# The second feed-forward's down projection: a two-level split into 49 products in place of a one-level split into 7

## The chip, the core and the metric

The kernel runs on one core of one Trainium2 chip, alone. The metric is the device time of one execution in microseconds. TensorE (PE) multiplies, VectorE (DVE) and ScalarE (ACT) work on vectors out of SBUF and PSUM, GpSimd (POOL) does vector work out of SBUF, and SyncE (SP) issues most of the DMAs. In the profile PEld is the load of TensorE's stationary operand, which has a row of its own.

## The reference

Everything is float32. There are 8 sequences of 512 tokens with 512 features, and a context of 64 rows a sequence. Two layers are computed, each a gated attention to the context and a gated feed-forward:

```python
x = x + tanh(g_xattn[0]) * linear_attention(layernorm(x), ctx, Wq, Wg, bg, Wkv, Wo)
x = x + tanh(g_ffn[0]) * (gelu(layernorm(x) @ proj1.T + b1) @ proj2.T + b2)          # 512 -> 2048 -> 512
x = x + tanh(g_xattn[1]) * softmax_attention(layernorm(x), ctx, mask)
# the second feed-forward: 8 experts of width 192, all of them used, weighted per token by a router
w_tg = top8_of_softmax_summed_by_group(layernorm(x) @ gate_weight.T)                  # token x expert
act  = silu(h_gate) * h_up          # h = layernorm(x) @ gate_up_proj[dominant].T
x = x + tanh(g_ffn[1]) * sum_g w_tg[:, g] * (act[:, g] @ down_proj[g].T)              # 512 -> 8*192 = 1536 -> 512
```

The change concerns the last line: per sequence a product of 512 x 1536 activations (already weighted by the router) with a 1536 x 512 matrix.

## The kernel before

The work runs in three phases of eight sequences each (`b` = 0 to 7): `xa0` (linear attention), `ff0` (first feed-forward) and `ff1` (second attention and second feed-forward). While the products of one sequence run, the preparation of the next (layer norm, transposes, in `ff1` also the whole second attention and the router) is fed in between, a step at a time; it is a generator, `prep`.

**Split products.** A matrix product is cut into 2 x 2 blocks on each side and done as seven block products in place of eight, with sums and differences of blocks formed beforehand (Strassen's scheme in Winograd's form). The seven are numbered 1 to 7; `ORDER = (1, 2, 6, 5, 7, 4, 3)` is the order in which they are issued. `Unit.step(m)` issues product `m` and then what follows it (`after`). Products add up in PSUM: `BANK` gives each one of three banks, x, w or z, and those in `OPENS` start a bank afresh. `steps` issues the last two products of a unit (4 and 3) only behind the first product of the next unit, so that other engines have time.

**Up units.** `Ff1Up` makes 256 columns of each of the four blocks of the activation; there are six per sequence, `i` = 0 to 5. Each of its seven products is four matmuls with 128 x 128 weights held and 256 tokens moving (L711). Even units fill the blocks `a11` and `a21`, odd ones `a12` and `a22`. After an odd unit `combine_inner` forms `s1`, `s2` and the new `a21` for these columns.

**Down unit.** `Down` is the unit of the change. For sequence `b` in `ff1` it has 6 chunks, so each of its seven products is 12 matmuls: 128 x 128 of the activation held, 256 columns of the weights moving (L823). `after` adds the bank straight into the residual `xb` with one DVE operation of 512 elements (L839), and updates `s2` after product 6 (L842).

**Weights.** The block combinations of the weights are the same for all sequences. They are formed once by `build_weights` on POOL and kept in DRAM (`store`), for `ff1` during the `ff0` phase. Tiles of 128 x 512 (256 KB) come back through a ring of 16 buffers in SBUF. Their loads stand on SP's queue in the order of use, 16 tiles ahead, each waiting for PE to be done with the buffer that it takes.

**What sets the order.** In `ff0` and `ff1` a scheduler of the language orders the instructions of each engine; each engine then runs its own in that order. PSUM has eight banks: three for `ps` (transposes and the like), five for the units' sums.

Of the kernel before, what the change touches and what calls it, by code (L numbers as in the profile page):

```python
# [30 lines left out]
P = 128  # L31
# [12 lines left out]
H2 = 256  # L44
# [24 lines left out]
def flamingo_kernel(  # L69
# [41 lines left out]

    def acc_bank(name):
        return bank["acc"].tile([P, 2, H2], F32, tag="acc", name=name)
# [149 lines left out]
    def order_gate():  # L263
# [9 lines left out]

    store = {
        (ph, kind, i, q): dram.tile([P, 2, H2], F32, tag=f"{ph}_{kind}{i}_{q}", name=f"{ph}_{kind}{i}_{q}")
        for ph, kind, n in (("ff0", "up", 4), ("ff0", "down", 4), ("ff1", "up", 6), ("ff1", "down", 3))
# [58 lines left out]
    def build_weights(ph, tile7):  # L335

        todo = {
            "ff0": (("up", raw_p1, 4), ("down", raw_p2, 4)),
            "ff1": (("up", raw_gu, 6), ("down", raw_dn, 3)),
        }[ph]  # L340
        todo = [(kind, raw, i) for kind, raw, n in todo for i in range(n)]

        def load(kind, raw, i):
            t = tile7(f"{ph}_{kind}{i}")
            raw(t, i)
            return t

        t = load(*todo[0])
        yield
        for n, (kind, raw, i) in enumerate(todo):  # L350
            following = load(*todo[n + 1]) if n + 1 < len(todo) else None
            yield from combining(nc.gpsimd, t)
            for q in range(7):
                nc.sync.dma_start(out=store[ph, kind, i, q], in_=t[q])
            yield
            t = following


    def normed(ph, b, tag):
# [26 lines left out]
        def turn(t):  # L386
            pt = psum(f"pt_{tag}_{t}").rearrange("p (c q) -> p c q", q=P)
            for c in range(NC):
                nc.tensor.transpose(pt[:, c, :], xn[t][:, ts(c, P)], ident)  # L389
            nc.scalar.copy(xnT[:, :, ts(t, P)], pt)  # L390
# [196 lines left out]
    def prep_ff1(b):  # L587
# [54 lines left out]
        for i in range(2):  # L642
            spread_share(b, i)
# [24 lines left out]
    OPENS = (1, 5, 2)  # L668

    class Unit:  # L670


        banks: dict

        def step(self, m):
            name = BANK[m]
            if m in OPENS:
                self.banks[name] = acc_bank(f"{name}_{self.tag}")
            self.product(m, self.banks[name])
            self.after(m, self.banks[name])  # L680

# [8 lines left out]
    class Up(Unit):  # L690
        kind = "up"

        def __init__(self, ph, b, i):
            self.ph, self.b, self.i, self.tag = ph, b, i, f"{ph}_{b}_{i}"
            self.banks, self.s = {}, {}
# [78 lines left out]

    class Ff1Up(Up):


        def part(self, r, c, p, s):
            if (r, c) == (1, 1):
                if self.i == 0:  # L780
                    open_inner("ff1", self.b, NJ // 2)
                self.g = {}
# [15 lines left out]
            else:  # L798
# [3 lines left out]
                if r == 2:  # L802
                    self.up22 = u
                else:
                    nc.vector.tensor_tensor(h, u, self.g[1], ALU.mult)
                    if self.i % 2:
                        combine_inner(ts(self.i // 2, 2))

    class Down(Unit):
        kind, i, prefix = "down", 0, ""  # L810

        def __init__(self, ph, b, chunks):
            self.ph, self.b, self.chunks, self.tag, self.banks = ph, b, chunks, f"{ph}_{b}_down", {}

# [15 lines left out]
        def after(self, m, p):  # L830

            xb = xs[self.ph, self.b]
            parts = {1: (1, 1), 2: (1, 1), 6: (1, 2), 7: (2, 2), 4: (2, 1), 3: (1, 2)}
            todo = [(parts[m], p)] if m in parts else []
            if m == 7:
                todo.append(((2, 2), self.banks["w"]))
            for (r, c), src in todo:
                dst = xb[:, ts(r - 1, 2), ts(c - 1, H2)]
                nc.vector.scalar_tensor_tensor(dst, src, GATE[self.ph], dst, ALU.mult, ALU.add)  # L839
            if m == 6:  # L840
                s2, a12 = self.inner["s2"], self.inner["a12"]
                nc.vector.tensor_tensor(s2, a12, s2, ALU.subtract)  # L842
            if m == 3:
                stores.append((self.ph, self.b))

# [119 lines left out]
    def steps(units, late=late):  # L965

        for u in units:
            for m in ORDER[:5]:
                yield u, m
                if m == 1:  # L970
                    yield from late
                    late.clear()
            late.extend((u, k) for k in ORDER[5:])
# [137 lines left out]
    def units_of(ph, b):  # L1111
        if ph == "ff0":
            return [Ff0Up(ph, b, i) for i in range(4)] + [Down(ph, b, NF // 2)]
        return [Ff1Up(ph, b, i) for i in range(6)] + [Down(ph, b, NJ // 2)]

    later = []
# [8 lines left out]
    def load_steps():  # L1125
        for u, m, _ in plan:
            key = (u.ph, u.kind, u.b, u.i, m)
            ring_w[key] = []
            for i in [u.i] if u.kind == "up" else range(u.chunks // 2):
# [3 lines left out]
                yield  # L1133

# [3 lines left out]
    for u, m in [*steps([ODown(B - 1)]), *late]:  # L1138
# [7 lines left out]
        acc=stack(tc.tile_pool(name="ff_acc", bufs=5, space=PSUM, reuse_waits="tile")),  # L1146
    )
    hpool = stack(tc.tile_pool(name="inner", bufs=1, reuse_waits="tile"))
# [16 lines left out]

    def build_tiles(name):
        t = buildp.tile([P, 7, 2, H2], F32, tag="build", name=f"build_{name}")
        return [t[:, q] for q in range(7)]
# [10 lines left out]
    for u, m, n in plan:  # L1179
        if n != at:  # L1180
# [5 lines left out]
            at, k, held = n, 0, False  # L1186
        u.step(m)
        for _ in range(1 if u.kind == "up" else u.chunks // 2):
            next(loads, None)
        k += 1  # L1190
        if k == 6:
            flush()
        if u.kind == "up" and u.ph == "ff1" and m == 5 and u.i < 4:
            spread_share(u.b, u.i + 2)
# [9 lines left out]
        if held:  # L1204
            if u.kind == "down" and u.b == work_list[n][1] and m == 2:
# [6 lines left out]
        if k * count // until > (k - 1) * count // until:  # L1212
            held = next(prep, None) == "last"
    flush()
    build.close()
# [44 lines left out]
```

## Time and profile before

| | |
|---|---|
| median of 3 runs | 2147.32 us (2147.06 to 2150.36) |
| the profiled execution's own time | 2149.09 us |
| its span, first to last instruction | 2147.3 us |
| PE matmul busy | 2116.5 us, 99% |
| PE weight load busy | 1798.6 us, 84% |
| DVE busy | 1068.6 us, 50% |
| ACT busy | 523.1 us, 24% |
| POOL busy | 225.9 us, 11% |
| DMA | 397.49 MB, mean 185 GB/s |

The last down projection of `ff1` ends with its matmuls at 2142 us, followed by one DVE operation and two stores of 256 KB. The granted clock of TensorE is 0.997 of full speed on average. Matmuls are pipelined: the record of one overlaps the next, so that time per matmul is read from the distance of starts, while the sum of a group counts overlaps once.

### The profile page before, as it was taken

To read this page: it belongs to the slowest core of one execution; us is meant where nothing else is said; L and a number is where in the kernel's file an instruction comes from. 1 tells how busy PE (TensorE), PEld (TensorE's weight loads), DVE (VectorE), ACT (ScalarE), POOL (GpSimd) and SP (SyncE) were. 2 spreads that over 40 slices of the span, in tenths; PEclk is the share of its full clock that TensorE was granted. 3 is DMA by queue.
4 is the path that set the end of the run, shared out by engine and by line. 5 is a ranking of instruction groups with operands and counts; after the bars stand their busy time and mean duration, and the time that the engine had idled before them with its cause. 6 is when DMAs were issued, how large, how long until landed. Compare 5 with 4: busy or idle time off the path is not lost.

```text
span 2147.3 us, 28078 instructions
## 1 busy us (share of the span) xinstructions
PE 2116.5 (99%) x10444; PEld 1798.6 (84%) x10444; DVE 1068.6 (50%) x1915; ACT 523.1 (24%) x1082; POOL 225.9 (11%) x216
## 2 busy tenths in 40 slices
PE   8999999999999999999999999999999999999998
PEld 4778787788888888888888888888888888888887
DVE  3687787543432324232334373747465573746453
ACT  3433333212130303132233221212121221213020
POOL 3121111332310101000000010100000010100000
PEclk9999999999999999999999999999999999999999
DMA  7345634699965655655555656565565666565662
GB/s 222 118 152 164 202 121 113 216 322 325 310 201 152 187 169 170 190 150 189 152 175 172 192 169 213 162 213 173 182 203 176 198 184 192 155 198 157 200 183 84
DMA packets 223880, 397.49 MB, mean 185 GB/s; under 512 B 32257, under 2 KB 54049, under 8 KB 219649
## 3 DMA queue, kind: packets, MB, share of 16 engines
q1 hardware_dynamic: 216304, 368.93, 55.2%
q10 hardware_dynamic: 5856, 23.20, 3.0%
q0 software_dynamic: 1584, 3.57, 0.7%
q8 instruction: 84, 1.38, 0.3%
q14 instruction: 52, 0.42, 0.1%
HBM read 335.97 MB, written 59.64 MB: 184 GB/s over the span
## 4 chain that ended last, share of the span: by engine, by line
PE 83%; issue 8%; DVE 3%; DMA 3%; POOL 1%; SPq 1%; ACT 1%; POOLq 0%; ACTq 0%
PE x_ff L711 25%; PE x_ff_down L823 18%; PE w_ff L711 13%; PE w_ff_down L823 9%; PE z_ff L711 6%; PE z_ff_down L823 5%; PE pt_ff L389 1%; PE pt_xa L389 1%; PE pr L580 1%; PE pst L538 1%; SPq L60 1%; PE x_q L711 1%; DMA w_v<-in_wkv 1%; PE x_xa_down L823 1%; POOL raw_ff_up L60 0%
## 5 line engine op out<-in xcount | busy, mean ns | idle before, releaser
L723 ACT COPY u_ff<-x_ff 128x512 f32<-128x512 f32 x240 | 139.8, 583 | 851.9 <-PE x_ff L711 851.7
L711 PE MATMUL w_ff<-S_ff,w_ff_up 128*128 128x256 f32 x1280 | 304.3, 380 | 0.0
L711 PE MATMUL x_ff<-S_ff,w_ff_up 128*128 128x256 f32 x1280 | 303.6, 380 | 0.6 <-ACT u_ff L723 0.6
L823 PE MATMUL x_ff_down<-w_ff_down,a_ff 128*128 128x256 f32 x1344 | 298.1, 379 | 0.8 <-DVE x_ff L839 0.8
L711 PE MATMUL x_ff<-xnT_ff,w_ff_up 128*128 128x256 f32 x1280 | 294.9, 380 | 0.0
L823 PEld LDWEIGHTS x_ff_down<-w_ff_down,a_ff 128*128 128x128 f32 x1344 | 255.2, 190 | 35.9 <-DVE x_ff L839 1.2
L711 PEld LDWEIGHTS x_ff<-xnT_ff,w_ff_up 128*128 128x128 f32 x1280 | 240.5, 190 | 38.0 <-issue 5.9
L711 PEld LDWEIGHTS w_ff<-S_ff,w_ff_up 128*128 128x128 f32 x1280 | 240.2, 190 | 38.0 <-issue 6.7
L711 PEld LDWEIGHTS x_ff<-S_ff,w_ff_up 128*128 128x128 f32 x1280 | 239.1, 190 | 35.6 <-issue 3.1
L823 PE MATMUL w_ff_down<-w_ff_down,s_ff 128*128 128x256 f32 x896 | 198.6, 379 | 0.0
L823 PEld LDWEIGHTS w_ff_down<-w_ff_down,s_ff 128*128 128x128 f32 x896 | 170.2, 190 | 23.1
L711 PE MATMUL z_ff<-xnT_ff,w_ff_up 128*128 128x256 f32 x640 | 151.8, 379 | 0.0
L839 DVE SCALAR_TENSOR_TENSOR x_ff<-x_ff_down,gates,x_ff 128x512 f32<-128x512 f32 x32 | 24.0, 752 | 231.6 <-PE x_ff_down L823 231.6
L711 PEld LDWEIGHTS z_ff<-xnT_ff,w_ff_up 128*128 128x128 f32 x640 | 119.3, 190 | 15.0
L839 DVE SCALAR_TENSOR_TENSOR x_ff<-x_ff_down,gates_half,x_ff 128x512 f32<-128x512 f32 x32 | 24.0, 751 | 164.9 <-PE x_ff_down L823 164.9
L823 PE MATMUL x_ff_down<-w_ff_down,s_ff 128*128 128x256 f32 x448 | 99.3, 379 | 0.0
L823 PE MATMUL z_ff_down<-w_ff_down,a_ff 128*128 128x256 f32 x448 | 99.3, 379 | 0.0
L823 PEld LDWEIGHTS x_ff_down<-w_ff_down,s_ff 128*128 128x128 f32 x448 | 85.1, 190 | 11.6
L823 PEld LDWEIGHTS z_ff_down<-w_ff_down,a_ff 128*128 128x128 f32 x448 | 85.1, 190 | 11.6
L766 DVE TENSOR_TENSOR a_ff<-w_ff,u_ff 128x512 f32<-128x512 f32 x64 | 43.8, 685 | 102.4 <-ACT u_ff L723 100.3
L801 DVE TENSOR_TENSOR up_ff<-w_ff,u_ff 128x512 f32<-128x512 f32 x96 | 66.0, 687 | 37.4 <-ACT u_ff L723 37.4
L510 POOL TENSOR_TENSOR x_ff<-x_ff,b_sb 128x512 f32<-128x512 f32 x28 | 35.9, 1286 | 422.9 <-DVE xn_ff L382 368.7
(221 smaller groups left out, 2491.0 us busy)
## 6 DMA issues: line engine op xcount, KB each, us to landing
w_ff_up<-ff_up SPq DMA_DIRECT2D x560, 256.0 KB
w_ff_down<-ff_down SPq DMA_DIRECT2D x392, 256.0 KB
x_ff<-x_ff SPq DMA_DIRECT2D x16, 1024.0 KB
share<-shares SPq DMA_DIRECT2D x64, 256.0 KB
ff_up<-build_ff_up SPq DMA_DIRECT2D x42, 256.0 KB
spread<-over SPq DMA_DIRECT2D x32, 256.0 KB
x_ff<-x_xa ACTq DMA_DIRECT2D x8, 1024.0 KB
x_ff<-x_ff ACTq DMA_DIRECT2D x8, 1024.0 KB
```

The costliest lines, as they stand in the source:

```text
L60: made = f(*args, **kw)
L389: nc.tensor.transpose(pt[:, c, :], xn[t][:, ts(c, P)], ident)
L510: nc.gpsimd.tensor_tensor(xb[:, t, :], xb[:, t, :], b2_sb, ALU.add)
L538: nc.tensor.matmul(pst[ts(r, M), :], lhsT=ctxT[:, c, :], rhs=xnT[:, c, :].rearrange("p (u r q) -> p r u q", u=2, r=2)[:, r], start=c == 0, ...
L580: nc.tensor.matmul(pr, lhsT=eT[half, t // 2, :], rhs=c2[half, :], start=True, stop=True)
L711: nc.tensor.matmul(p[:, n, :], lhsT=w[:, c, ts(n, P)], rhs=moving, **self.mark(m, 2 * n + c),)
L723: nc.scalar.copy(self.s[m], p)
L766: nc.vector.tensor_tensor(h, p, s, ALU.add)
L801: nc.vector.tensor_tensor(u, p, s, ALU.add)
L823: nc.tensor.matmul(p[:, t, :], lhsT=a[:, k, ts(t, P)], rhs=w[k // 2][:, k % 2, :], **self.mark(m, 2 * k + t),)
L839: nc.vector.scalar_tensor_tensor(dst, src, GATE[self.ph], dst, ALU.mult, ALU.add)
```

## The change

In `ff1` the down unit becomes `SplitDown`. Each of its seven block products is itself cut into 2 x 2 quarters and done as seven products of quarters: 49 in all, of three matmuls each, with 128 x 128 of the activation held and 128 columns of weights moving.

- Each inner product has 128 columns of PSUM of its own; the seven of an outer product lie side by side in two banks, four and three. The outer sums are made on these seven separately: in PSUM along x and w, and otherwise in a tile `sums`, filled by ACT (`first`) and added to by DVE (`more`).
- The inner scheme's last sums and the addition into the residual are made once per sequence, by `whole`: three additions and eight operations into `xb`, put off (`pending`) and issued four per step. In the last sequence they are done in three parts.
- The activation's quarters are combined by DVE right before each outer product: `combine(m)`, four operations of 384 elements, into two buffers `split`. `combine(1)` is called in two places.
- The outer products come in the order 2, 4, 1, 6, 5, 7, and 3 behind the next unit's first product. The units of `ff1` come odd first, `FF1_UNITS`, since products 2 and 4 use `a12` and `a22`. Tokens of the normed input are placed in another order, so that the quarters come out right.
- The weights are one DRAM tensor, `stream`, in order of use: 147 blocks of 128 x 128 for each sequence, read as 37 ring tiles where there were 21. `build_stream` makes it on POOL: three tiles with four operations of 512 elements as before and four of 896 more, and 21 stores in pieces of 512 bytes.
- The five banks of the units' sums have fixed numbers, and are handed out in the order in which they fall idle.

```diff
+    SPLIT_ORDER = (2, 4, 1, 6, 5, 7, 3)
+    SPLIT_INNER = (1, 2, 4, 5, 6, 7, 3)
+    SPLIT_CHUNKS = NJ // 4
+    stream = dram.tile([P, 7, 7, SPLIT_CHUNKS, P], F32, tag="stream", name="stream")
...
+    def build_stream(tile7):
+        place = [SPLIT_ORDER.index(m) for m in (1, 5, 2, 3, 6, 7, 4)]
+        for i in range(SPLIT_CHUNKS):
+            t = tile7(f"ff1_down{i}")
+            w = [t[k] for k in place]
+            raw_dn(w, i)
+            yield
+            yield from combining(nc.gpsimd, w)
+
+            t = buildp_view(t)
+            more = buildp_view(tile7(f"ff1_split{i}"))
+            m = {
+                1: t[:, :, 0, 0], 5: t[:, :, 0, 1], 2: t[:, :, 1, 0], 3: t[:, :, 1, 1],
+                6: more[:, :, 0, 0], 7: more[:, :, 0, 1], 4: more[:, :, 1, 0],
+            }
+            for dst, a, b in ((7, 3, 5), (5, 5, 1), (6, 3, 5), (4, 2, 6)):
+                nc.gpsimd.tensor_tensor(m[dst], m[a], m[b], ALU.subtract)
+                yield
+            for n, k in enumerate(SPLIT_INNER):
+                nc.sync.dma_start(out=stream[:, :, n, i, :], in_=m[k])
+            yield
...
+            at = t % 2 * 2 + t // 2 if tag.startswith("ff1") else t
+            nc.scalar.copy(xnT[:, :, ts(at, P)], pt)
...
+    FF1_UNITS = (1, 0, 3, 2, 5, 4)
...
+    class SplitDown(Unit):
+        kind, i = "down", 0
+        order, head = SPLIT_ORDER, 6
+        BANK = {2: "z", 4: "v", 1: "x", 6: "x", 7: "x", 5: "w", 3: "w"}
+        OPENS, CLOSES = (2, 4, 1, 5), (2, 4, 7, 3)
+        NAMES = {1: "a11", 2: "a12", 4: "a22", 5: "s1", 6: "s2", 7: "a21", 3: "s2"}
...
+        def combine(self, m):
+            a = self.quarters(m)
+            s = second.tile([P, 4, self.chunks, P], F32, tag="split", name=f"split{m}_{self.tag}", bufs=2)
+            nc.vector.tensor_tensor(s[:, 0], a["21"], a["22"], ALU.add)
+            nc.vector.tensor_tensor(s[:, 1], s[:, 0], a["11"], ALU.subtract)
+            nc.vector.tensor_tensor(s[:, 2], a["11"], a["21"], ALU.subtract)
+            nc.vector.tensor_tensor(s[:, 3], a["12"], s[:, 1], ALU.subtract)
+            self.combined[m] = s
+
+        def product(self, m, p):
+            a, s = self.quarters(m), self.combined.pop(m)
+            w = ring_w[self.ph, self.kind, self.b]
+            operand = {1: a["11"], 2: a["12"], 4: a["22"], 5: s[:, 0], 6: s[:, 1], 7: s[:, 2], 3: s[:, 3]}
+            for n, k in enumerate(SPLIT_INNER):
+                for c in range(self.chunks):
+                    at = (SPLIT_ORDER.index(m) * 7 + n) * self.chunks + c
+                    nc.tensor.matmul(
+                        p[n // 4][:, n % 4, :],
+                        lhsT=operand[k][:, c, :],
+                        rhs=w[at // 4][:, ts(at % 4, P)],
+                        start=m in self.OPENS and n % 4 == 0 and c == 0,
+                        stop=True,
+                        skip_group_check=True,
+                    )
+
+        def after(self, m, p):
...
+            def first(part):
+                nc.scalar.copy(self.sums[part][:, 0:4], p[0])
+                nc.scalar.copy(self.sums[part][:, 4:7], p[1][:, 0:3])
+
+            def more(part):
+                for at, src in ((slice(0, 4), p[0]), (slice(4, 7), p[1][:, 0:3])):
+                    dst = self.sums[part][:, at]
+                    nc.vector.tensor_tensor(dst, src, dst, ALU.add)
+
+            if m in (2, 4, 6, 5):
+                first({2: (1, 1), 4: (2, 1), 6: (1, 2), 5: (2, 2)}[m])
+            if m == 7:
+                more((2, 2))
+                more((2, 1))
+            if m in (1, 3):
+                more({1: (1, 1), 3: (1, 2)}[m])
+            if m == 6:
+                nc.vector.tensor_tensor(inner["s2"], inner["a12"], inner["s2"], ALU.subtract)
...
+        def whole(self, r, c):
...
+            return [
+                onto(6, 1), out_of(1, 0, 0), out_of(2, 0, 0), onto(5, 6), out_of(5, 0, 1), out_of(3, 0, 1),
+                out_of(5, 1, 1), out_of(7, 1, 1), onto(7, 6), out_of(7, 1, 0), out_of(4, 1, 0), done,
+            ]
...
-        return [Ff1Up(ph, b, i) for i in range(6)] + [Down(ph, b, NJ // 2)]
+        return [Ff1Up(ph, b, i) for i in FF1_UNITS] + [SplitDown(ph, b, NJ // 4)]
...
         u.step(m)
-        for _ in range(1 if u.kind == "up" else u.chunks // 2):
+        for _ in range(tiles_of(u, m)):
             next(loads, None)
+        for _ in range(4):
+            if pending:
+                pending.pop(0)()
+        if isinstance(u, Ff1Up) and u.i == FF1_UNITS[-1]:
+            if m == 2:
+                down_of[u.b].combine(2)
+                down_of[u.b].combine(4)
+            if m == 3:
+                down_of[u.b].combine(1)
+        if isinstance(u, SplitDown) and m in (4, 1, 6, 5, 7):
+            u.combine(SPLIT_ORDER[SPLIT_ORDER.index(m) + 1])
```

## The prediction

> **What bounds the kernel now.** I read the page first: its busy rows, then the chain.
>
> ```profile
> PE 2116.5 (99%) x10444; PEld 1798.6 (84%) x10444; DVE 1068.6 (50%) x1915; ACT 523.1 (24%) x1082; POOL 225.9 (11%) x216
> ...
> PE 83%; issue 8%; DVE 3%; DMA 3%; POOL 1%; SPq 1%; ACT 1%; POOLq 0%; ACTq 0%
> ...
> q1 hardware_dynamic: 216304, 368.93, 55.2%
> ```
>
> TensorE (PE) is busy for 99% of the span and carries the chain. Only PE time, or a new wait of PE, moves the end. The waits of PE in the second feed-forward (from 1216 us) come to one line, in the last batch:
>
> ```profile
> PE x_ff_down L823 <- DVE x_ff L839: 0.8, 1, 0.8
> ```
>
> Then the PE timeline of one down projection (ff1, the fourth of eight), and that of the kernel's first microseconds:
>
> ```profile
> 1428.34 1.89 PE L711 MATMUL x_ff<-xnT_ff,w_ff_up 128*128 128x256 f32 x8
> 1430.07 5.34 PE L823 MATMUL x_ff_down<-w_ff_down,a_ff 128*128 128x256 f32 x24
> 1435.25 5.34 PE L823 MATMUL w_ff_down<-w_ff_down,s_ff 128*128 128x256 f32 x24
> 1440.43 0.60 PE L389 MATMUL pt_xa<-ident,xn_xa 128*128 128x128 f32 x4
> 1440.87 1.46 PE L711 MATMUL z_ff<-xnT_ff,w_ff_up 128*128 128x256 f32 x6
> ...
> 1.07 2.93 PE L60 MATMUL idle<-zeros 128*128 128x128 f32 x12 [1.07 <-DVE heads L60]
> 3.79 1.06 PE L60 MATMUL pctx<-ident,ctx 128*128 128x128 f32 x4
> ```
>
> Every product written in the code runs as two passes (12 matmuls of a down product are x24, six idle ones x12); a transpose runs as one. From 1430.07 to 1435.25 are 5.18 us for 24 passes: 215.8 ns a pass of 256 columns. The starts count, since a row's length includes a drain that overlaps the next. Four transposes of 128 columns take 0.44 us, 109 ns each, and each loads its own 128x128 weights.
>
> **The products.** Per batch 84 products of 256 columns (7 of 12) become 147 of 128 columns (49 of 3). Before: 7 x 5.18 = 36.26 us. After: 294 passes, and the question is what a pass of 128 columns costs when each needs a fresh load of 128 columns. The load's record is 190 ns, longer than the whole 109 ns. But at 1440.00 us such a load starts 2 ns after the matmul before it, is on record to 1440.19, and the next matmul starts on its 215.8 ns: it lies beside the matmul. Whether it fits beside a matmul half as long is shown by the idle row: plain products with plain loads of 128 columns, each spaced 213 ns by their starts. The transposes pctx just behind them are spaced (1.06 - 0.42) / 3 = 213 ns too, against 109 at 1440 us, so PE ran there at half speed (512-column passes start 853 ns apart at 10 us, 429 ns at 18 us), and the load hid completely. At full speed that is 107 to 109 ns. Bounds: 107, and 190 if the load's whole record were bare. I take 109.3: 294 x 0.1093 = 32.13 us. Saved: 4.13 us a batch, **33.0 us** over eight. (At 110 ns it would be 31.4.)
>
> One rule speaks against this. The Trainium skill, "TensorE: Matmul & The Clock Gate", Part 3, says that a weight load overlaps running matmuls only where its row group differs; all rows here use all 128 rows. With that page's 107 ns a load, load and matmul in series would be an estimated 214 ns a pass and the change some 210 us slower. The trace disagrees already for 256 columns, as the load that starts 2 ns behind its matmul shows.
>
> **DVE work added.** Rows of ff1: tensor_tensor 128x256 425 ns, 128x512 685, 128x1536 1748, scalar_tensor_tensor 128x512 751. So 384 columns take about 555. In the DVE timeline independent 512-column operations start 600 ns apart (83 ns overlap), and one that needs the operation just before it 720; for 384 columns 470 and 590. Per batch: eight combinations of four operations, though only seven are used (the code forms that of product 1 twice: behind the last up unit and again behind product 4), 8 x 2.0 = 16 us; eight additions out of PSUM, 4.6; the outer sums, three additions and eight scalar_tensor_tensor, 7.2; less seven old ones, 5. That is some 23 us, two thirds of it in the down projection itself. There DVE has room, as the stretch of the same down projection shows (columns: PE, PEld, DVE, ACT, POOL busy, clock, DMA share, GB/s):
>
> ```profile
> 1398.99:1440.43 41.44, 41.44 (x194) 36.43 (x192) 14.79 (x21) 1.77 (x3) 0.00 (x0) 1.00 0.65 202
> ```
>
> DVE is busy 14.8 of 41.4 us. ACT gets eight copies a batch, about 4.2 us, and does 1.8 us there.
>
> Beside PE this costs nothing unless a product waits. I walk through the order in which the changed program puts DVE's instructions. V is the end of the last up product; PE to DVE takes 0.2 us (product ends 2142.37, DVE starts 2142.57), back about 0.05. From V, DVE does the up part (0.2), two inner products, s1, the first (unused) combination of product 1, s2, a21, then the used combination. Its first member is ready at 6.5, the second at 7.4. PE does product 4 to 4.6, then nine matmuls of product 1 that need no combination (1.97) to 6.6, three with the first member to 7.2: it waits 0.2. Four token combinations of the next batch follow on DVE, then product 1's addition from 10.2 to 10.9; product 6 writes the same bank. The program fills 1.3 us with six matmuls of product 5, to 10.7: wait 0.2. Product 6 ends at 15.5; s2's update (1.75 us, needs product 6 done) stands ahead of the third member of product 5's combination, which comes at 18.0 where PE wants it at 17.5: wait 0.5. Products 7 and 3 find theirs early. Behind product 3 the outer sums delay the next unit's parts, but its bank is wanted at 42.1 and read by 40.0. Sum 0.9 us a batch, **+7.2 us**. Bounds: 0 (nothing excludes an idle DVE being ahead), and above, one wait as long as the one in the trace (1.0 us from product to product) at each of four products, 4 us a batch. I take the walk, since it uses rows of the very same operations.
>
> **The end.** Now the last product's one DVE operation (0.75 us) stands before two stores. In the changed program the w1 addition (0.6) and thirteen small operations stand there, three of 256 columns (0.35 to 0.45) and ten of 128 (about 0.25; row 128x128: 292 ns): 4.2 us. **+3.4 us**; stores as before. The old 1.0 us wait of the last batch goes, and one of about 1.0 comes there, since four small operations stand ahead of product 5's second member.
>
> **Weights.** Down needs 37 tiles of 256 KB a batch for 21. From its first to its last product run 40 tiles and some 1.3 MB of shares in about 37 us: 315 GB/s. The page's queue row makes 55.2% x 16 x 2147.3 us / 216304 = 88 ns for 1706 bytes, 311 GB/s with all engines busy, and slices of the page reach 325. The ring holds 16 tiles, 4.2 MB, loaded ahead, and the up units behind need only one tile in 1.73 us. So a shortfall down to about 205 GB/s is covered: 0. A piece stays 2 KB, but rows now lie 75 KB apart in DRAM, which no row here shows. SP's queue: stores of the output wait for the outer sums some 5 us later, ring loads behind them; the ring's lead of 27 us in up units covers that.
>
> **The build** runs in ff0: 12 POOL operations more, of 896 columns (about 2.25 us from the row 1286 for 512), and 21 stores in 512-byte pieces, 9.6 MB for 5.5. PE, DVE and ACT orders are unchanged there. SP waits for POOL with ring loads queued behind, a few us against the 27 us lead; DMA is at 85 to 96% there and PE did not wait. 0, at most 5 us.
>
> The rest (another token order, odd units first, banks named by number) has the same instructions: 0.
>
> **Sum.** The profiled execution took 2149.1 us (span 2147.3), 1.8 over the median. 2149.1 - 33.0 + 7.2 + 3.4 = 2126.7; against the median, 2125.
>
> **Rivals.** (1) Slower: the weight load does not fit behind a matmul of half its length. For: 190 ns on record, and no row shows a plain load of 128 columns with a plain matmul of 128 at full speed. Against: the idle row. It decides from (290.1 - 10.6) / 2352 = 119 ns a pass; at 130 the kernel takes 2173, at 190 2314. (2) DVE lags: the walk has margins of a few tenths, and one late operation delays all behind it. From 2 to 4 us a batch: 2134 to 2150, about no change at 2.8 us more than the walk. (3) The stream starves: below 205 GB/s, as 131 GB/s (200 ns a packet) would make it, PE waits in each down for 11.8 - 4.2 - 4.9 = 2.7 MB, 20 us a batch: 2280. Against it, every piece is as long as before. (4) It doesn't do what it says: by count 7/8 of 290.1 us saves 36.3, so 3.3 are lost to the fixed 2 to 3 ns of a pass; only the unused combination is waste.
>
> **How the numbers follow.** The forecast (2115 to 2137) 0.65; rival 2 (2137 to 2151) 0.13; rival 1 0.12; rival 3 0.06; the build hurting by over 5 us 0.04, still faster. A difference of 0.2%, 4.3 us, is about what a measurement of this kernel can tell from none. Faster, below 2143: 0.65 + 0.04 + half of rival 2. Low end: no waits at all and 107 ns, 2125 - 7.2 - 4; the high end takes in rival 2, and leaves out about 0.2.
>
> **What would show it.** Passes of the split product 109 ns apart; PE waits on DVE of 0.2 to 0.5 us at products 1, 6 and 5, about 7 us in all; none on DMA; DVE near 70% busy in down; the end of the chain on DVE for 4 to 5 us. Wrong if passes are over 119 ns apart, or PE waits over 3.7 us a batch.

## The result, and the profile after

The changed kernel takes 2149.95 us (median of 12 runs, 2147.12 to 2153.86) beside 2148.93 (2146.01 to 2153.79, 12 runs) for the one before: ratio 1.0003 [0.9994, 1.0012], no change. The forecast was 2125, range 2113 to 2150, with about 0.06 for no change (half of rival 2). The profiled execution took 2147.87 us (span 2146.1) for 2149.09 (2147.3) before, so 1.2 us is what has to be accounted for in the two traces.

The page of the changed kernel, busy rows, chain and ring queue:

```profile
PE 2094.4 (98%) x11452; PEld 1807.5 (84%) x11452; DVE 1242.7 (58%) x2289; ACT 557.0 (26%) x1146; POOL 251.0 (12%) x228
...
PE 79%; issue 8%; DVE 6%; DMA 4%; POOL 2%; SPq 1%; ACT 1%; ACTq 0%; POOLq 0%; DVEq 0%
...
q1 hardware_dynamic: 250864, 406.10, 60.0%
```

PE has 22 us less work, and the span is 1.2 us shorter: PE now waits. The chain shows more DVE, DMA and POOL in place of PE. PE's waits from 1216 us on (`ff1`), then the longest from 400 to 1216 us (mainly `ff0`) in the changed kernel and in the one before (columns: engine, tile and line, what was waited for, us in total, times, longest):

```profile
PE pt_ff L425 <- DVE xn_ff L418: 4.5, 5, 0.9
```

```profile
PE x_ff L752 <- ACT u_ff L764: 15.6, 4, 11.4
```

```profile
PE x_ff L711 <- ACT u_ff L723: 0.6, 1, 0.6
```

The 15.6 us lie in the *first* feed-forward. The longest of the four waits ends at 617.71 us, and the first split product starts at 1296. That is where most of the saving went.

The down projection itself, as the PE timeline has it (start, length, instruction, tile of the group's first), fourth sequence:

```profile
1425.83 2.17 PE L939 MATMUL x_ff_down<-w_ff_down,a_ff 128*128 128x128 f32 x18
1427.84 3.10 PE L939 MATMUL x_ff_down<-w_ff_down,split_ff_down 128*128 128x128 f32 x24
1430.78 1.50 PE L939 MATMUL w_ff_down<-w_ff_down,s_ff 128*128 128x128 f32 x12
1432.12 2.24 PE L939 MATMUL x_ff_down<-w_ff_down,s_ff 128*128 128x128 f32 x18
1434.20 2.84 PE L939 MATMUL x_ff_down<-w_ff_down,split_ff_down 128*128 128x128 f32 x24
```

Twelve passes from 1430.78 to 1432.12 are 111.7 ns each, and so are most others. A group with operands that DVE makes shows a wait: 24 passes from 1427.84 to 1430.78 are 2.94 us for 2.68. The stretch as a whole (columns: PE, PEld, DVE, ACT, POOL busy, clock, DMA share, GB/s):

```profile
1413.00:1451.30 38.30, 38.28 (x320) 37.50 (x319) 29.99 (x55) 6.18 (x12) 0.00 (x0) 1.00 0.93 303
```

38.30 us for 41.44, at full clock, with no wait for weights. DVE is busy 30.0 of 38.3 us, 78%.

From here the time of each phase is read from PE alone. The *ff0 stretch* runs from the first matmul of the first down projection of `ff0` to that of the last: 700.42 us before, **718.67** after, although PE has the very same work there. The *ff1 stretch*, between the same points of `ff1`, is 821.31 before and **805.13** after. What lies ahead of these stretches varies by itself: the first down projection of `ff0` starts at 445.63, 446.62, 447.83 and 448.00 us in four kernels below that differ only in `ff1`. So a difference of 2 us between two profiled times says little. The ff0 stretches of these four lie within 0.9 us (701.51 to 702.44), so the stretches are compared.

### The profile page after: what moved, and what is told of

It is laid out like the page before. It is cut to its first block, busy times and chain, and to the rows that moved or that the text cites. A ratio compares the mean times of both kernels' runs of the same rounds, so it can differ in the third digit from the quotient of the medians.

```text
span 2146.1 us, 30885 instructions
## 1 busy us (share of the span) xinstructions
PE 2094.4 (98%) x11452; PEld 1807.5 (84%) x11452; DVE 1242.7 (58%) x2289; ACT 557.0 (26%) x1146; POOL 251.0 (12%) x228
## 4 chain that ended last, share of the span: by engine, by line
PE 79%; issue 8%; DVE 6%; DMA 4%; POOL 2%; SPq 1%; ACT 1%; ACTq 0%; POOLq 0%; DVEq 0%
PE x_ff L752 24%; PE w_ff L752 12%; PE x_ff_down L868 10%; PE z_ff L752 6%; PE x_ff_down L939 5%; PE w_ff_down L868 5%; PE w_ff_down L939 3%; PE z_ff_down L868 3%; PE z_ff_down L939 2%; PE v_ff_down L939 2%; PE pt_ff L425 1%; PE pt_xa L425 1%; PE pr L618 1%; PE pst L576 1%; DMA x_ff<-x_ff 1%
## 5 line engine op out<-in xcount | busy, mean ns | idle before, releaser
L868 PE MATMUL x_ff_down<-w_ff_down,a_ff 128*128 128x256 f32 x768 | 169.7, 379 | 0.0
L868 PEld LDWEIGHTS x_ff_down<-w_ff_down,a_ff 128*128 128x128 f32 x768 | 145.8, 190 | 19.8
L868 PE MATMUL w_ff_down<-w_ff_down,s_ff 128*128 128x256 f32 x512 | 113.1, 379 | 0.0
L868 PEld LDWEIGHTS w_ff_down<-w_ff_down,s_ff 128*128 128x128 f32 x512 | 97.2, 190 | 13.2
L812 ACT ACTIVATE a_ff<-a_ff,b_sb 128x256 f32<-128x256 f32 x128 | 58.1, 500 | 92.2 <-DVE a_ff L807 92.2
L791 DVE TENSOR_TENSOR s_ff<-a_ff,a_ff 128x512 f32<-128x512 f32 x56 | 40.2, 718 | 58.1 <-ACT a_ff L812 57.9
L939 PE MATMUL x_ff_down<-w_ff_down,split_ff_down 128*128 128x128 f32 x576 | 70.1, 276 | 0.2
L939 PEld LDWEIGHTS x_ff_down<-w_ff_down,split_ff_down 128*128 128x128 f32 x576 | 66.8, 192 | 1.5 <-issue 1.5
L837 DVE TENSOR_TENSOR g_ff<-g_ff,share 128x512 f32<-128x512 f32 x96 | 65.9, 686 | 2.1
```

Source lines behind the costliest of these rows:

```text
L791: nc.vector.tensor_tensor(s1, a21, a22, ALU.add)
L812: nc.scalar.activation(h[:, n, :], p[:, n, :], AF.Gelu, bias=b1_sb[:, f : f + 1])
L837: nc.vector.tensor_tensor(g, g, share, ALU.mult)
L868: nc.tensor.matmul(p[:, t, :], lhsT=a[:, k, ts(t, P)], rhs=w[k // 2][:, k % 2, :], **self.mark(m, 2 * k + t),)
L939: nc.tensor.matmul(p[n // 4][:, n % 4, :], lhsT=operand[k][:, c, :], rhs=w[at // 4][:, ts(at % 4, P)], start=m in self.OPENS and n % 4 == ...
```

## The experiments

Where an expectation speaks of theories, they are those on record with it. All ratios are to the kernel before; "ff0" and "ff1" are the stretches just named.

| kernel | median us (range, runs) | ratio | ff0 | ff1 |
|---|---|---|---|---|
| changed | 2149.95 (2147.12 to 2153.86, 12) | 1.0003 [0.9994, 1.0012] | 718.67 | 805.13 |
| stream stores on POOL's queue | 2152.03 (2150.50 to 2155.86, 10) | 1.0019 [1.0010, 1.0029] | 721.58 | |
| SP in program order | 2132.03 (2130.43 to 2134.24, 4) | 0.9924 [0.9905, 0.9943] | 701.77 | 805.15 |
| residual store on POOL's queue | 2150.99 (2149.79 to 2154.14, 10) | 1.0012 [1.0003, 1.0022] | 719.94 | |
| before, more bytes | 2148.99 (2145.11 to 2154.11, 10) | 1.0001 [0.9991, 1.0011] | 704.47 | |
| before, more POOL time | 2170.84 (2169.70 to 2170.85, 4) | 1.0103 [1.0084, 1.0121] | 724.94 | 821.31 |
| in order, one combination less | 2130.05 (2128.88 to 2131.57, 4) | 0.9920 [0.9902, 0.9937] | 701.51 | 804.70 |
| the same, 22 steps | **2126.50** (2123.01 to 2127.68, 4) | 0.9897 [0.9877, 0.9917] | 702.44 | 799.08 |
| the same, residual loads free | 2130.85 (2129.37 to 2132.09, 4) | 0.9916 [0.9897, 0.9935] | 706.84 | 799.08 |
| changed, store on POOL, one combination less, 22 steps | 2144.68 (2142.01 to 2147.48, 10) | 0.998 [0.9971, 0.999] | 720.41 | 799.08 |

Three more were run once each, so their times have no interval: half the columns 2154.18, one combination twice over 2135.92, and a ring of 12 tiles 2135.87 us.

**Where the wait in `ff0` comes from.** SP's own waits for POOL in the changed kernel, 400 to 700 us (SPq is SP's queue of DMA issues), then the longest such wait in the kernel before:

```profile
SPq L391 <- POOL build_ff_down L241: 17.4, 3, 6.8
SPq L391 <- POOL build_ff_split L388: 16.0, 3, 6.7
```

```profile
SPq L354 <- POOL build_ff_up L231: 3.9, 2, 3.5
```

SP stands 33.4 us at the stores of the stream (L391) until POOL is done with a tile: 17.4 us for the four operations of 512 columns that were there before (the last is L241), and 16.0 for the four of 896 columns that the build now has besides (L388). Before, it stood 5.9 us for POOL from 400 to 720 us, now 36.6. The first experiment moves those stores to POOL's queue:

```diff
-                nc.sync.dma_start(out=stream[:, :, n, i, :], in_=m[k])
+                nc.gpsimd.dma_start(out=stream[:, :, n, i, :], in_=m[k])
```

> Changed kernel, but the 21 stores of the stream are issued on POOL's queue, right behind the POOL operations that make the tiles, and not on SP's queue. Same bytes, same 512-byte pieces. Theory A (SP stands still on POOL's operations, 17.4 + 16.0 us in the waits of SP from 400 to 700 us, with ring loads queued behind it): the gap of 11.4 us at 606 us and the clock's dip behind it go, the phase ff0 is 16 to 18 us shorter, 2132 to 2135 us. Theory B (the 4.1 MB more of stores fill the DMA engines): the gap stays, about 2150 us.

Measured 2152.03, ff0 721.58: the expected gain did not come. SP's waits for POOL fell to 2.6 us, but another took their place (the same window of SP's waits):

```profile
SPq L340 <- DMA stream<-build_ff_split: 32.6, 4, 17.8
```

The raw loads of the next tile (L340, the weights from which POOL forms the combinations) need a buffer that the stores must have left. There are two build buffers, and the split quarters now take the second. So SP still stands at one build instruction, and ACT stands 29.3 us for the raw loads, as it does 29.5 in the changed kernel (shown further below). The second experiment changes not where the stores are issued but what may be queued behind them: SP stays in the order of the code through `ff0`, where the code has the stores some steps after POOL's work, in place of the scheduler's order.

```diff
-            if n > B:
+            if n >= 2 * B:
                 in_order.clear()
```

> Changed kernel, but SP's queue is kept in the order of the program through all of ff0, where the stores of a stream tile stand some steps behind the POOL operations that it needs, so that SP should find POOL done. Theory A: as with the stores on POOL's queue, 2132 to 2135 us, waits of SP for POOL near 0. Theory B: a gap of about 10 us stays somewhere in ff0, 2145 to 2150 us, unless the wider spacing of the stores hides it.

Measured 2132.03, ff0 701.77, 16.9 us less than in the changed kernel and 1.4 more than before; ff1 is unchanged at 805.15. SP waits for POOL nowhere in 400 to 720 us, and the long wait of PE is gone:

```profile
PE x_ff L752 <- ACT u_ff L764: 1.2, 1, 1.2
```

So the loss is the build's, and it is a matter of SP's order. The kernel before has little to gain from such an order: its PE waits from 400 us to the end add up to 2.2 us.

**Bytes or POOL's time?** The build also stores more (9.6 MB for 5.5, in 512-byte pieces). Two kernels made from the one before add each part alone. More bytes:

```diff
                 nc.sync.dma_start(out=store[ph, kind, i, q], in_=t[q])
+                if ph == "ff1" and kind == "down":
+                    part = t[q].rearrange("p n (h q) -> p (n h) q", q=P)[:, 0:3]
+                    nc.sync.dma_start(out=extra[:, q, :, i, :], in_=part)
```

> Kernel before, with 21 more stores in ff0, of 192 KB each in 512-byte pieces into a tensor that nobody reads: the 4.1 MB that the changed kernel stores more, without its twelve more POOL operations. Theory A (the wait of SP for POOL is what hurts): no change, 2146 to 2151 us. Theory B (the bytes are what hurts; 4.1 MB at 311 GB/s are 13 us of all engines): 2157 to 2165 us.

2148.99, ratio 1.0001 [0.9991, 1.0011]: in the time the bytes can't be told from nothing. In its one profile ff0 is 4.05 us longer, and PE waits 4.3 us for ACT there, so they may have a small part; not a large one, since the kernel with SP in order stores the same bytes with ff0 1.4 us over before. More POOL time (a quarter is added and then subtracted again, so the weights stay as they were but for rounding):

```diff
             yield from combining(nc.gpsimd, t)
+            if ph == "ff1" and kind == "down":
+                v = whole[id(t[0])].rearrange("p k n (h q) -> p k n h q", q=P)
+                for n in range(2):
+                    for op in (ALU.add, ALU.subtract):
+                        nc.gpsimd.tensor_tensor(v[:, :, n, 0], v[:, :, n, 0], v[:, :, n, 1], op)
+                        yield
```

> Kernel before, with four POOL operations of 896 columns more on each of the three tiles of the old down weights, ahead of their stores (a quarter is added and subtracted again): POOL's 8.6 us a tile of the changed kernel, with the old bytes, the old stores and the old two buffers that take turns. Theory D1 (POOL's time alone makes SP stand): SP waits for POOL 25 us or more between 400 and 700 us, PE has a gap of 10 us or more, 2160 us or more. Theory D2 (it also takes the second buffer, which in the changed kernel holds the split quarters, so that the next tile's loads start only behind the stores): SP waits for POOL under 15 us, no gap above 3 us, 2147 to 2152 us.

2170.84, 22.5 us slower than before in the same runs, with the down projection untouched (ff1 821.31) and ff0 24.5 us longer, more than the 18.25 of the changed kernel. Its SP, PE and ACT repeat the pattern of the changed kernel:

```profile
SPq L362 <- POOL build_ff_down L359: 35.2, 3, 12.2
```

```profile
PE x_ff L719 <- ACT u_ff L731: 19.4, 3, 16.6
```

```profile
622.19 0.58 ACT L731 COPY u_ff<-x_ff 128x512 f32<-128x512 f32 x1 [36.05 <-DMA w_ff_up<-ff_up]
```

**How SP's wait reaches PE.** Not through weights that come late, which the prediction had named: PE waits for ACT. PE's timeline at the gap (in brackets: idle time of the engine, and what ended it), then ACT's (ACTq is its queue of DMA issues), then the first of the four new operations on POOL, in the changed kernel:

```profile
605.72 0.60 PE L425 MATMUL pt_ff<-ident,xn_ff 128*128 128x128 f32 x4
617.71 3.64 PE L752 MATMUL x_ff<-S_ff,w_ff_up 128*128 128x256 f32 x8 [11.40 <-ACT u_ff L764]
```

```profile
616.71 0.33 ACTq L170 DMA_DIRECT2D x_ff<-x_ff  x1
617.07 0.59 ACT L764 COPY u_ff<-x_ff 128x512 f32<-128x512 f32 x1 [29.51 <-DMA build_ff_down<-in_dn]
```

```profile
589.93 2.07 POOL L388 TENSOR_TENSOR build_ff_split<-build_ff_down 128x896 f32<-128x896 f32 x1
```

ACT stood 29.5 us at an instruction that is no computation: its issue of the store of a residual (L170). In the trace that issue waits for a semaphore (a counter that a finished DMA raises) on which it counts together with one of SP's raw loads for the third build tile. The load was issued only at 613.09, since SP stood behind POOL; it had landed at 616.55, and ACT's issue follows at 616.71. The copy `u_ff` queued behind the store is what PE needs. In the kernel with more POOL time ACT stands 36.0 us at the same store, there for a ring load that SP issued late. The Trainium skill, "DMA: Bandwidth & Descriptors", in "Anatomy of one DMA", a section on DMAs that GpSimd issues, says that a DMA engine waits for no semaphore and that any such wait happens on the issuing sequencer before dispatch. Here the issuer is ACT, and this trace agrees: 29.5 us of ACT with no work between.

If that were the only way, moving this one store off ACT's queue would mend it:

```diff
-            nc.scalar.dma_start(out=between[{"xa0": "ff0", "ff0": "ff1"}[ph], b], in_=t)
+            queue = nc.gpsimd if ph == "ff0" else nc.scalar
+            queue.dma_start(out=between[{"xa0": "ff0", "ff0": "ff1"}[ph], b], in_=t)
```

> Changed kernel, with one edit: the store of a sequence's residual at the end of its ff0 work is issued on POOL's queue and not on ACT's. The build, its stores and SP's order stay as the changed kernel has them. Theory C (new: the gap at 606 us is ACT's own queue, which stood 29.5 us, to 616.7 us, at this store, waiting for the completion count that the store shares with SP's loads for the third build tile, the last of them issued at 613.1 us; ACT's copy of an up product, for which PE waits, is queued behind it): the gap goes, 2131 to 2135 us, with ACT's wait of 29.5 us gone. Theory A (ring loads late behind SP's waits): no change, 2147 to 2152 us.

2150.99, ff0 719.94: a miss. ACT no longer stands there, and PE waits all the same, 16.8 us up to 637.09 (PE's waits, then DVE's timeline and ACT's):

```profile
PE x_ff L753 <- ACT u_ff L765: 18.0, 2, 16.8
```

```profile
632.62 1.29 DVE L405 BATCH_NORM_STATS2 st_ff<-x_ff 128x6 f32<-128x512 f32 x2 [21.80 <-DMA x_ff<-x_ff]
```

```profile
635.66 0.91 ACT L813 ACTIVATE a_ff<-a_ff,b_sb 128x256 f32<-128x256 f32 x2 [21.80 <-DVE a_ff L808]
```

Now DVE stands 21.8 us at the statistics of a later sequence, for a residual load that SP issued at 625.26, again late. Behind the statistics on DVE stands `a_ff` (634.92), for which ACT waits 21.8 us (635.66); behind that on ACT stands `u_ff` (636.48), for which PE waits. Two engines' queues held an instruction that depended on SP; freeing one hands the stall to the other.

**The passes.** Is the pace of 111.7 ns the matmul's or its weight load's? In the second and third matmul of each product only 64 of 128 columns are moved (their other columns are left out of the sums):

```diff
+                    cols = P if c == 0 else P // 2
                     nc.tensor.matmul(
-                        p[n // 4][:, n % 4, :],
+                        p[n // 4][:, n % 4, 0:cols],
                         lhsT=operand[k][:, c, :],
-                        rhs=w[at // 4][:, ts(at % 4, P)],
+                        rhs=w[at // 4][:, at % 4 * P : at % 4 * P + cols],
```

> Changed kernel, with only 64 of 128 columns moved in the second and third matmul of each of the 49 products: the other 64 columns of these terms are left out. Theory L (a load of 128 columns of weights takes 111.7 ns and sets the pace): passes stay 111 to 112 ns apart, the down projection's 33 us too. Theory F (a pass costs its columns and some 5 ns): passes of 64 columns 58 ns apart, down projection 22.5 us where the weights arrive in time.

The first product of the fourth sequence in this kernel's PE timeline, and in that of the changed kernel:

```profile
1413.49 2.12 PE L940 MATMUL z_ff_down<-w_ff_down,a_ff 128*128 128x128 f32 x18
1415.45 2.84 PE L940 MATMUL z_ff_down<-w_ff_down,split_ff_down 128*128 128x128 f32 x24
1418.13 1.95 PE L752 MATMUL x_ff<-xnT_ff,w_ff_up 128*128 128x256 f32 x8
```

```profile
1413.00 2.17 PE L939 MATMUL z_ff_down<-w_ff_down,a_ff 128*128 128x128 f32 x18
1415.01 2.84 PE L939 MATMUL z_ff_down<-w_ff_down,split_ff_down 128*128 128x128 f32 x24
1417.69 1.89 PE L752 MATMUL x_ff<-xnT_ff,w_ff_up 128*128 128x256 f32 x8
```

42 passes take 4.64 us with a third fewer columns moved, and 4.69 with all of them. Of six starts of matmuls in turn one comes 58 ns and one 165 ns behind the start before it, the others 111 to 112, while the loads keep their 111.7. The weight load sets the pace: it runs beside the passes, and half the columns do not shorten it. The Trainium skill, "TensorE: Matmul & The Clock Gate", section "LDWEIGHTS", gives columns over 1.2 as the nanoseconds of a load, an estimated 107 for 128 columns; the runs show 111.7.

**DVE in the down projection.** One of the eight combinations is unused. It is left out:

```diff
-        if isinstance(u, SplitDown) and m in (4, 1, 6, 5, 7):
+        if isinstance(u, SplitDown) and m in (1, 6, 5, 7):
```

> The kernel with SP in order, and the combinations of product 1 formed only once, behind the last up unit: four DVE operations (2 us) less in each sequence. If they are hidden beside PE but for the end of the chain to product 1 (0.18 + 0.07 us of gaps there, 0.07 at product 6): these 0.3 us a sequence go, 2.5 us in all, about 2129.5 us; the 0.9 us wait of the transposes for the next sequence's normed input stays. Rival (DVE lags as a whole, so that the late normed input comes from the combinations too): that wait goes as well, about 2124.5 us.

2130.05 for 2132.03, near the 2129.5 expected, but by luck: ff1 went only from 805.15 to 804.70, 0.06 us a sequence for 0.3, and most of the difference of the two profiles lies ahead of `ff0` (2.4 of 3.3 us). The PE gaps over 111.7 ns went from 295, 184 and 179 ns in three places to 268 and 213 in two: product 1's operand came earlier, and product 6 then waited for product 1's addition. The opposite, the second forming of product 1's combinations done twice over (the new argument is how often the four operations are issued), costs:

```diff
-            u.combine(SPLIT_ORDER[SPLIT_ORDER.index(m) + 1])
+            u.combine(SPLIT_ORDER[SPLIT_ORDER.index(m) + 1], 2 if m == 4 else 1)
```

> The kernel with SP in order, with the second forming of product 1's combinations done twice over: four more DVE operations (1.9 us) a sequence ahead of the combination's last result and of what follows it. If the margins of the walk hold to a few tenths: PE's gaps at product 1 grow from 0.25 by about 0.9 to 1.9 us, with the additions behind it late by the same, 7 to 15 us more in all, 2139 to 2147 us. Rival (DVE's idle time in the down projection, 8 of 38 us, takes it up): under 0.5 us a sequence, 2132 to 2136 us.

ff1 809.65, 4.5 us more, 0.64 a sequence for about 2 us of DVE work: the time (2135.92, one run) is in the rival's range, the 0.64 between the two expectations. Inconclusive as to price, since the scheduler answered by another order of matmuls, and of PE's new waits in `ff1` 3.6 us were for weights and 0.6 for DVE.

**The transposes.** The 0.9 us of `pt_ff <- xn_ff` remained in both. DVE's timeline in the changed kernel around it:

```profile
1494.88 0.17 DVE L405 BATCH_NORM_AGGREGATE mv_ff<-st_ff 128x2 f32<-128x6 f32 x1
...
1496.81 0.69 DVE L849 TENSOR_TENSOR a_ff<-up_ff,g_ff 128x512 f32<-128x512 f32 x1
1497.41 0.17 DVE L409 TENSOR_SCALAR var_ff<-mv_ff 128x4 f32<-128x4 f32 x1
1498.73 1.00 DVE L418 TENSOR_SCALAR xn_ff<-x_ff,mv_ff,rstd_ff 128x512 f32<-128x512 f32 x2 [0.56 <-POOL rstd_ff L411]
```

The small operation `var_ff` stands behind the operations of an up unit, and the next sequence's norm comes just too late for PE. How many steps of preparation are fed in per sequence sets that place:

```diff
-        return 5 if ph == "ff0" else 21 if b else 23
+        return 5 if ph == "ff0" else 22 if b else 23
```

> As the kernel with the combinations of product 1 formed once, and the preparation of the next sequence in the second feed-forward cut for 22 steps where it was 21, so that it comes a little earlier and DVE's operation on the variances stands ahead of an up unit's five operations and not behind them. If that order makes the wait for the normed input (0.9 us, five sequences, with the restart 1.07 each): 5.3 us less than with the combinations formed once, about 2124 us. Rival (DVE has too much to do before it, whatever the order): no change to that kernel.

2126.50, the fastest of all, 1.0% below the kernel before. ff1 fell by 5.6 us for the 5.3 expected. `var_ff` follows soon behind the statistics, PE has no wait left in `ff1` that the view lists, and each of the first six distances from one down projection to the next is 115.58 us (in the changed kernel five are 116.73 to 116.77, the sixth 115.65). DVE's timeline of this kernel:

```profile
1475.50 0.30 DVE L405 BATCH_NORM_AGGREGATE mv_ff<-st_ff 128x2 f32<-128x6 f32 x2
1476.31 0.15 DVE L409 TENSOR_SCALAR var_ff<-mv_ff 128x4 f32<-128x4 f32 x1
```

**The stream's margin.** Ring of 12 tiles for 16, else as the second experiment:

```diff
-    RING = 16
+    RING = 12
```

> The kernel with SP in order, and a ring of 12 weight tiles in place of 16. The down projection takes 40 tiles in 38 us at 300 GB/s and a DMA share of 0.92. If the lead of the ring is what covers that: PE waits for weights in each down projection, 1 to 5 us each, 2140 to 2170 us. Rival (the DMA keeps up with PE there without a lead): no wait for weights in the second feed-forward, 2130 to 2136 us.

2135.87 in one run, in the rival's range, but ff1 is 810.12, 5.0 us more, and PE waits for weights, four times and not in each down projection (1210 to 2140 us):

```profile
PE w_ff_down L939 <- DMA w_ff_down<-stream: 3.7, 4, 1.1
```

The lead of 16 tiles does cover the down projection, with less than four tiles to spare. With 16 tiles two other kernels show such waits in `ff1` too: 3.6 us with the combination done twice over, 2.4 with half the columns.

**Two tries at a better version.** The changed kernel, SP left in the scheduler's order, with three of the edits above: the residual store off ACT, one combination less, and 22 steps:

```diff
-            nc.scalar.dma_start(out=between[{"xa0": "ff0", "ff0": "ff1"}[ph], b], in_=t)
+            queue = nc.gpsimd if ph == "ff0" else nc.scalar
+            queue.dma_start(out=between[{"xa0": "ff0", "ff0": "ff1"}[ph], b], in_=t)
...
-        return 5 if ph == "ff0" else 21 if b else 23
+        return 5 if ph == "ff0" else 22 if b else 23
...
-        if isinstance(u, SplitDown) and m in (4, 1, 6, 5, 7):
+        if isinstance(u, SplitDown) and m in (1, 6, 5, 7):
```

> Changed kernel with three edits: the residual's store of ff0 on POOL's queue, product 1's combinations formed once, 22 preparation steps. If these three are what the change lost beside its 111.7 ns passes: 17 + 0.5 + 5.6 us below the changed kernel, and without the 3 us that SP in order leaves in ff0: 2122 to 2125 us. Rival (the late build loads hold up something else once ACT is free): 2126 us or more.

2144.68, the rival's case: ff1 is at the best value, 799.08, and ff0 keeps its loss (720.41), with DVE 23.5 us at one residual load. And the fastest kernel with the residual loads released from SP's kept order:

```diff
-        queue = nc.scalar if ph == "xa0" and b > 1 else nc.sync
+        queue = nc.scalar if ph == "xa0" and b > 1 else nc.sync if ph == "xa0" else tc.nc.sync
```

> The kernel with SP in order, product 1's combinations formed once and 22 preparation steps, with one more edit: the loads of the residual are left out of the order that SP is held to, so that they stand 15 to 40 entries earlier on its queue. If the 3 us that are left in ff0 come from DVE, which stands behind a late residual load with an up unit's operations queued behind its statistics: 2123 to 2124 us, every ff0 sequence 98.45 us. Rival (they come from DMA that is short there): no change, 2126.5 us.

2130.85, 4.3 slower: DVE then waits 17.1 us for residual loads (15.1 in the fastest kernel), and PE 4.2 us up to 943.98 us. Missed; the fastest kernel's 2.0 us over before in ff0 stay open. A third build buffer was not tried.

## Why the prediction was wrong

Term by term, in profiled microseconds:

| term of the sum | predicted | measured |
|---|---|---|
| passes of the down products | -33.0 | -27.4: 8 x (294 x 0.11167 - 36.26) |
| PE's waits for DVE in down | +7.2 | +2.5 |
| end | +3.4 | +3.1 |
| the old 1.0 us wait of the last sequence | 0 | -1.0 |
| transposes for the next sequence's norm | not named | +5.6 |
| the build in `ff0` | 0, at most 5 | **+18.25** |
| start and between phases | 0 | -2.3 |
| sum | -22.4 | -1.2 |

The -2.3 is no effect of the change: the start differs as much between kernels that are equal there.

- **The step that failed: "SP waits for POOL with ring loads queued behind, a few us against the 27 us lead … 0, at most 5 us."** SP's wait was 33.4 us, not a few: the stores of a tile wait for eight POOL operations, four of them new, of about 2.08 us each. With the stores out of SP's way, its next wait was as long (32.6 us), for the second buffer, which the quarters take. And the ring loads were not the victims; PE did not wait for weights there. The victims were engines whose own queues held an instruction tied to SP: ACT at a store, and DVE at a residual load once the store was moved. The store on ACT's queue cost PE 11.4 us in one wait, of its 15.6. The prediction asked who waits for SP's *data in the ring* and not who else waits for anything SP issues late. It also took "PE, DVE and ACT orders are unchanged there" for "their times are unchanged". The kernel before with POOL's time added has the loss too (+24.5 us in ff0), and SP in order removes it from the changed one (+1.4): the cause is shown by both.
- **The second step: the walk through DVE's order** stopped at the down projection. Its three waits were found at products 1 and 6, at 0.32 us a sequence (0.25 in the last) for 0.9 predicted; the one at product 5 was not there. Not walked was the next sequence's normed input, 1.28 us from the matmul before to the first of four transposes where there were 0.22, and 0.06 to the second, five times: +5.6. Undone by one more step of preparation.
- **A mis-sized term: the pass.** 109.3 ns was the distance of two transposes, whose loads are 141 ns on record where those of the products are 190; 111.7 is the pace of the latter, 2.4 ns more over 2352 passes, 5.6 us. The idle row, halved, would have been 106.5; why the load is slower than that at full speed, no run shows. Rival 1's point, 119 ns, was not reached.
- **Right:** the end (last matmul's start to the span's end 8.27 us for 5.17), no starving (303 GB/s needed and got; rival 3 fell), DVE beside PE, though busier (78% for near 70%).
- **Two slips without effect:** 107 ns a pass would be 5.4 us below 109.3, not 4, and 20 us a batch would make rival 3's time about 2285, not 2280.

The end, in the timeline of the changed kernel, as forecast on DVE:

```profile
2135.22 2.84 PE L939 MATMUL w_ff_down<-w_ff_down,split_ff_down 128*128 128x128 f32 x24
2138.14 0.55 DVE L961 TENSOR_TENSOR sums_ff_down<-w_ff_down,sums_ff_down 128x384 f32<-128x384 f32 x1
...
2142.01 0.74 DVE L991 SCALAR_TENSOR_TENSOR x_ff<-sums_ff_down,gates_half,x_ff 128x128 f32<-128x128 f32 x2
```

The measured time lies in rival 2's range (2137 to 2151), but by luck and not by rival 2's way: the waits inside the down projection were smaller than the walk, not larger. The build case, given 0.04 at "over 5 us, still faster", was the one that decided.

## What to carry to other kernels

When a change adds work to an engine off the path, follow every instruction that waits for it, then every instruction queued behind *those*, and every one that shares a buffer or a completion count with them, in each engine's queue; a lead in one ring covers that ring alone. A stalled queue is mended where the queue is ordered: moving single DMAs to other queues handed the stall on twice (2152.03 and 2150.99 us), while issuing the stores later than the work they wait for removed it (2132.03). And a saving in one phase is read from that phase's own stretch of PE, or a loss elsewhere hides it: here -16.2 and +18.3 us.

## What the runs showed of the hardware that was not expected

Weight loads of 128 columns, 192 ns each on record, start 111.7 ns apart beside matmuls of 128 columns, with all rows used by both. Moving 64 columns in two matmuls of three gains almost nothing (42 passes in 4.64 us for 4.69).

The longest wait cost more than its length. Behind the 11.4 us gap the granted clock is down, by the windows of the changed kernel:

```profile
612.00:618.00 6.00, 0.29 (x1) 0.29 (x2) 0.00 (x0) 0.93 (x3) 0.00 (x0) 0.50 0.96 290
618.00:624.00 6.00, 6.00 (x22) 5.01 (x22) 0.69 (x1) 2.79 (x7) 0.21 (x1) 0.74 1.01 334
```

The clock is 0.50 in the first window and 0.74 in the second, and the eight passes behind the gap take 3.48 us where eight at 215.8 ns are 1.73: another 1.75 us. Six of them start 426 or 427 ns apart.
